# Spreading the shared experts of a scan-and-mixture kernel anew, with a rebuilt head and Silu on ScalarE

## The chip, the cores and the metric

The kernel runs on one core of a Trainium2 chip. The metric is the device time of one execution in microseconds (us), lower is better; a kernel's time is the median of its runs.

## What is computed

Input x has 8 batches of 512 tokens with 256 features, all in fp32. Two layers run one after the other, each followed by the same mixture of experts with the same weights:

```
x = x + scan_layer(layernorm(x))
x = x + mixture(layernorm(x))
x = x + causal_attention(layernorm(x))      # 16 heads of 16, scores clipped to +-10
x = x + mixture(layernorm(x))

scan_layer(x):  xi = silu(x @ Win + bin)                  # 256 -> 512
                h_t = 0.9 * h_(t-1) + xi_t * Bp           # state of 16 per feature
                y = sum_i(h * Cp) + Dp * xi ;  return y @ Wout + bout
mixture(x):     scores = sigmoid(x @ router.T)            # 16 experts in 4 groups
                keep the 2 best groups, then the 4 best experts; weights normalised, times 2.5
                routed = sum over the 4 of weight * down_e(silu(x @ gate_e) * (x @ up_e))
                shared = (silu(x @ sh_gate) * (x @ sh_up)) @ sh_down     # 2 shared experts
                return routed + shared
```

Because the decay is one constant, the scan keeps one state per inner feature and multiplies it by bc = sum(Bp * Cp) afterwards.

## The kernel before

**Stages.** The program has four stretches: the scan layer together with the first mixture's routing and shared experts (`stretch(Scan())`), the routed experts of the first mixture (`routed(0, ...)`), attention with the second mixture's routing and shared experts (`stretch(Attention())`), and the second mixture's routed experts. Between the first two lies no barrier but data: the routed experts need all 4096 tokens sorted into rows by expert.

**A stretch.** `stretch` loops over the batches. In each turn of the loop several pieces of work are written out interleaved, by `beside`: the main work of batch b (for the scan: `Scan.main`), the shared experts of batch b - 2, the routing of batch b - 1 (`Route`), the sends of batch b - 2's tokens, and the norm and transposition of batch b + 1. `beside` weaves pieces by matmul columns; `timed(steps, places...)` puts each step of a piece at a fraction of the turn. The order so written is the order on every engine's queue, and engines run their queues in order. What is listed behind the loop (the rest of the shared experts, the last batch's routing, the table of blocks) makes up the tail of the stretch.

**Scan.main.** For each of 4 chunks of 128 inner features: two matmuls of 512 columns into PSUM (`pz`, L532), sigmoid on ScalarE (L541), times its argument on VectorE (L542), the scan on VectorE (L544), the D skip on ScalarE (L545) and the sum on VectorE (L548). Then `add_projection` multiplies by Wout (`py_s`, L486) and adds to x (L495) in two halves.

**Route.** The norm of batch b (L444, L445; power by GpSimd, L464; rows `sorted_m`, L469), transposition by TensorE (`pt_m`, L406) with copies to `xT_m` (L408), router matmuls (`pl_m`, L630), transposition to `logit_m` (L641), sigmoid (`score_m`, L645), the choice of groups and experts by some forty small VectorE instructions (L656 to L744), counts by matmuls with a triangle and with ones (`pr_m`, L708 and L709), `where_m` (L716), slots cast by ScalarE in pairs (L756; for the last batch by VectorE in one copy, L738) and 16 indirect DMAs from GpSimd that send rows to their places in DRAM (L759). Behind the last batch come the zero fills of the unused ends (16 DMAs on SyncE), and the table of blocks (`pe_b` L871, `pl_b` L880, `lines_b`), which tells `routed` which expert each block of 128 rows has.

**Shared experts.** `shared_experts(i, b, ...)` yields 12 steps per batch: 8 of gate and up (4 matmuls each 128x512 per pair, `pg_m`, L1108), and 4 of down (`pd_m`, L1137); behind each pair come a sigmoid on ScalarE (L1126) and two products on VectorE (L1127, L1128), or a tanh form in attention. `HELD = 6`: in the last turn 6 steps of the batch are issued, the rest behind the loop. The transposed rows `xT_m` live in a pool of nine tiles (tag `kb4`).

**Routed experts.** For each block of 128 rows: gate and up matmuls (`ph`, L994), sigmoid on ScalarE (L1002), two products on VectorE (L1004, L1005), down matmuls (`pyr`, L1025), a gain on ScalarE (L1034) and an indirect DMA that adds the rows to the result (L1035). Expert weights are all resident in one tile, `w_all`, 3072 columns for each of 16 experts; in the scan stretch `later` holds their loads, which are issued on SyncE behind the loads of x.

**Head.** Constants are made by GpSimd; norms 0 and 1 take the inverse root by 13 VectorE instructions of Newton steps (`first`, `pinned`); `first_two` writes out batch 0's and batch 1's chunks. `load_shared` loads the shared weights.

Of the kernel before, what the change touches and what calls it, by code (L numbers as in the profile page):

```python
# [15 lines left out]
P = 128  # L16
# [47 lines left out]
HELD = 6  # L64
AHEAD = 6
BY_PE = 3

# [15 lines left out]
def tile_hybrid_block(  # L83
# [88 lines left out]
    load_x(0)  # L172
    ident = const.tile([P, P], FP, name="ident")
    make_identity(nc, ident)

# [13 lines left out]
    nc.scalar.dma_start(out=w_out_sb, in_=w_out.rearrange("(c p) d -> p c d", p=P))  # L189
    b_out_sb = const.tile([P, D], FP, name="b_out_sb")  # L190
    nc.gpsimd.dma_start(out=b_out_sb, in_=b_out.partition_broadcast(P))
    load_x(1)

    rw_sb = const.tile([P, KD, SQ], FP, name="rw_sb")
    nc.gpsimd.memset(rw_sb, 0.0)
    nc.gpsimd.dma_start(out=rw_sb[:, :, 0:E], in_=router_t.rearrange("(p k) e -> p k e", p=P))
    rb_sb = const.tile([P, E], FP, name="rb_sb")
    nc.gpsimd.dma_start(out=rb_sb, in_=route_bias.partition_broadcast(P))
# [24 lines left out]
    def load_expert(e: int):  # L223
# [11 lines left out]
    nc.gpsimd.memset(before, 1.0)  # L235
    nc.gpsimd.affine_select(
        out=before,
        in_=before,
        compare_op=ALU.is_gt,
        fill=0.0,  # L240
        base=0,
        pattern=[[1, EG], [-1, EG]],
        channel_multiplier=0,
    )
    neg_half = const.tile([P, NT], FP, name="neg_half")
    nc.gpsimd.memset(neg_half, -0.5)
# [4 lines left out]
    nc.scalar.activation(begun, decay, AF.Sigmoid)  # L251
# [6 lines left out]
    def load_attention_weights():  # L258
# [14 lines left out]
    nc.gpsimd.memset(causal, TOP)  # L273
    nc.gpsimd.affine_select(
        out=causal, in_=causal, compare_op=ALU.is_ge, fill=0.0, base=0, pattern=[[0, 2], [1, P]], channel_multiplier=-1
    )
# [3 lines left out]
    nc.gpsimd.memset(tri, 1.0)  # L280
    nc.gpsimd.affine_select(
        out=tri, in_=tri, compare_op=ALU.is_gt, fill=0.0, base=0, pattern=[[1, P]], channel_multiplier=-1
    )
    ones = const.tile([P, P], FP, name="ones")
    nc.gpsimd.memset(ones, 1.0)
# [4 lines left out]
    for e in range(E):  # L290
        nc.gpsimd.memset(region[:, e : e + 1], float(e * REG))
    steps = const.tile([P, NJ], FP, name="steps")
    nc.gpsimd.iota(steps, [[BLK, NJ]], base=0, channel_multiplier=0, allow_small_or_imprecise_dtypes=True)
# [29 lines left out]
    nc.gpsimd.memset(zeros, 0.0)  # L323
    nc.gpsimd.iota(zeros[:, D + 2 * TK :].bitcast(I32), [[0, SAME]], base=NTOK, channel_multiplier=1)


    later = [lambda e=e: load_expert(e) for e in range(E)]
# [62 lines left out]


# [45 lines left out]
    def normed(b: int, tag: str, place, by_vector: bool = False, pinned: bool = False, past=lambda: None):  # L437
# [10 lines left out]
        if by_vector:  # L448


            var = small.tile([P, NT], FP, tag="var", name=f"var_{tag}", bufs=1)
            keep(nc.vector.tensor_scalar(var, mv[:, :, 1], EPS, None, ALU.add))
            bits = small.tile([P, NT], I32, tag="bits", name=f"bits_{tag}", bufs=1)
            keep(nc.vector.tensor_scalar(bits, var.bitcast(I32), 1, None, ALU.logical_shift_right))
            keep(nc.vector.tensor_scalar(rstd.bitcast(I32), bits, -1.0, HALVED, ALU.mult, ALU.add))
            off = small.tile([P, NT], FP, tag="off", name=f"off_{tag}", bufs=1)
            for _ in range(3):
                keep(nc.vector.tensor_mul(off, rstd, rstd))
                keep(nc.vector.scalar_tensor_tensor(off, off, -0.5, var, ALU.mult, ALU.mult))
                keep(nc.vector.scalar_tensor_tensor(rstd, off, 1.5, rstd, ALU.add, ALU.mult))  # L460
            yield
        else:
            nc.vector.tensor_scalar(rstd, mv[:, :, 1], EPS, None, ALU.add)
            nc.gpsimd.tensor_tensor(rstd, rstd, neg_half, ALU.pow)  # L464
# [33 lines left out]
    class Scan:  # L498
        mixture, ahead, copies, turns = 0, 1, by_scalar, (0.75, 0.79)
        early = 0  # L500
# [5 lines left out]
        def load(self, b: int):  # L506
            if b + 1 < B and b > 0:
                with tc.issue_after(load_x(b + 1).ins):
                    for load in later[b - 1 :: shares]:
                        load()  # L510

# [12 lines left out]
        def main(self, b: int, xnT):  # L524
            tag = f"s{b}"

            def steps():
                y_sb = []
                for c in range(NI):
# [11 lines left out]
                    nc.scalar.activation(xi, pz, AF.Sigmoid, bias=bias)  # L541
                    nc.vector.scalar_tensor_tensor(xi, pz, bias, xi, ALU.add, ALU.mult)  # L542
# [38 lines left out]

    class Route:
# [3 lines left out]
        def __init__(self, i: int, b: int, copies):  # L586
            self.i, self.b, self.tag, self.copies = i, b, f"m{i}_{b}", copies
            self.held = {}
            self.rest = choices(i, b, self.tag, self.held, b < B - 1)
# [17 lines left out]
        def scores(self, shares: bool = False):  # L607
            if shares:
# [9 lines left out]
                self.copies,  # L618
                past=wide if self.i == 0 and self.b == B - 2 else None,
# [275 lines left out]
    def routed(i: int, table, beside):  # L895
# [90 lines left out]
        def up(n: int):  # L986
# [15 lines left out]
            nc.scalar.activation(act, ph[0], AF.Sigmoid)  # L1002
            with tc.issue_after(turns.pop(n + 1).ins) if n + 1 in turns else nullcontext():
                nc.vector.tensor_mul(act, ph[0], act)  # L1004
            made = nc.vector.tensor_mul(act, ph[1], act)  # L1005
# [43 lines left out]
        def run(first: int, last: int):  # L1049
# [13 lines left out]
            nc.scalar.activation(primed, decay, AF.Sigmoid)  # L1063
# [29 lines left out]
    def shared_experts(i: int, b: int, xnT_of, tanh: bool):  # L1093
# [3 lines left out]
        def steps():  # L1097
            xnT = xnT_of()
            acts = []
            for n in range(NSH):  # L1100
# [3 lines left out]
                for f in range(KF):  # L1104
# [20 lines left out]
                    else:  # L1125
                        nc.scalar.activation(sig, ph, AF.Sigmoid)  # L1126
                        nc.vector.tensor_mul(sig, ph, sig)  # L1127
# [35 lines left out]
    class Attention:  # L1163
        mixture, ahead, copies, turns = 1, 2, by_both, (0.65, 0.85)
        early = 2
        norms, scores, choose = (0.0, 0.12, 0.2, 0.28), (0.29, 0.45, 0.55, 0.6), (0.66, 0.95)
        last_rows, last_scores = (0.2, 0.28), (0.35, 0.38)
        bursts, parts = {}, {}

# [210 lines left out]
    def stretch(layer):  # L1380
# [5 lines left out]
        def norm(b: int, first: bool = False):  # L1386
# [4 lines left out]
            return normed(b, f"l{i}_{b}", place, first, first)  # L1391
# [13 lines left out]
        def experts(b: int):  # L1405
            return shared_experts(i, b, lambda: routes.pop(b).held["xnT"], i == 1)

        for b in range(layer.ahead):
            if b < layer.early:
                xT[b] = ready.pop(b)  # L1410
            else:
# [3 lines left out]
                issue(Piece(0, turn(b, by_both if first else layer.copies)))  # L1415
                if first:
                    load_shared()
            if b == 0:
                issue(project(b))

        def first_two():

            layer.load(1)
            issue(Piece(0, norm(1, True)))
            for _ in range(2):
                pending.pop(0)()
            main = layer.main(0, made.pop(0))
            issue(Piece(0, some(main.steps, NI)))
            issue(Piece(0, turn(1)))
            issue(project(1))  # L1430
            second = layer.main(1, made.pop(1))
            issue(Piece(0, some(second.steps, NI)))
            issue(main)
            return Piece(second.columns - NI * KD * T, second.steps)
# [9 lines left out]
        for b in range(1 if begun else 0, B):  # L1444
            pieces = [begun or layer.main(b, made.pop(b))]
            begun = None
            nxt, last = b + layer.ahead, b == B - 1
            fill = []
            if layer.ahead > 1 and not last:
                fill.append(project(b + 1))  # L1450
            if b > 1:
                shared_sum = experts(b - 2)
                if last:

                    each = shared_sum.columns // 12
                    rest = Piece((12 - HELD) * each, shared_sum.steps)

                    many = HELD * each if layer.mixture else HELD * each * 3 // 2
                    shared_sum = Piece(many, some(shared_sum.steps, HELD))
# [4 lines left out]
            if b > 0:  # L1464
# [13 lines left out]
                else:  # L1478
                    pieces += [
                        timed(r.scores(i == 1), *layer.scores[:2], *spread(*layer.scores[2:], NT)),  # L1480
                        timed(some(r.rest, PICKS), *spread(*layer.choose, PICKS)),
                    ]
            if nxt < B:
                added = layer.load(nxt)
                if added is not None:
# [4 lines left out]
                    timed(turn(nxt), *layer.turns),  # L1490
# [4 lines left out]
            if i == 0 and b == 2:  # L1495
# [10 lines left out]
                behind(rest, experts(B - 2)),  # L1506
# [9 lines left out]
                experts(B - 1),  # L1516
# [104 lines left out]
```

## Time and profile before

| what | us |
|---|---|
| median of 3 runs (lowest, highest) | 1681.23 (1679.09, 1684.41) |
| the profiled execution: its time | 1674.03 |
| its span, first to last instruction | 1672.1 |
| first matmul of a routed expert | 366.87 |
| scan stretch, 80 to 240 us: busy time of TensorE, VectorE, ScalarE, GpSimd per 40 us | 40.0, 34.6, 12.1, 23.7 |
| attention stretch with its tail, 745 to 1278 us: TensorE busy | 498.08 |
| second routed stretch, 1278 to 1660 us: TensorE busy | 378.08 |

PE is TensorE's matmuls, PEld its weight loads, DVE VectorE, ACT ScalarE, POOL GpSimd, SP SyncE, which only starts DMAs. A busy PE is one that has matmuls in flight. A wait is put down to the instruction whose semaphore came last. The granted clock is the share of full speed that the throttle left to TensorE. The four values of the fourth row are means of the four windows from 80 to 240 us.

### The profile page before, as it was taken

Reading aid. Unit: us, or ns where it says so; the run is one execution under the profiler, and the core shown is the slowest. Engines: PE = TensorE matmul, PEld = TensorE weight load, DVE = VectorE, ACT = ScalarE, POOL = GpSimd, SP = SyncE. Lnnn points to the kernel's source line nnn. Section 1 sums busy time; section 2 is a strip of 40 time slices with the busy share of each in tenths; the row PEclk is TensorE's granted clock in tenths of the full one; section 3 lists DMA queues with packets and bytes.
Section 4 is the critical chain, followed back from the end, with each engine's and each line's share of the span. In section 5 each row is a group of like instructions: output and inputs, shape, how many; then the busy total and the mean of one; then the engine's idle time right before and its main releaser. Section 6 shows DMA issues by size and latency. Waiting matters only on the chain.

```text
span 1672.1 us, 34224 instructions
## 1 busy us (share of the span) xinstructions
PE 1572.9 (94%) x9992; PEld 1156.6 (69%) x9992; DVE 1159.7 (69%) x3623; ACT 745.4 (45%) x1461; POOL 758.1 (45%) x655
## 2 busy tenths in 40 slices
PE   6999996979999999999999999999787999999996
PEld 3566663659999999984444454454356999999996
DVE  7988876436677766656888978978754566666664
ACT  3222332125555555546544443444213555555553
POOL 3365663525555555550023423422552555555554
PEclk9999998989999999999999999999899999999998
DMA  5354431527777766641333423332643767777776
GB/s 166 127 192 170 135 110 60 186 75 106 107 124 122 104 99 99 99 57 42 89 93 107 121 85 117 96 96 90 210 170 72 110 113 113 137 136 136 134 135 133
DMA packets 281645, 195.31 MB, mean 117 GB/s; under 512 B 168592, under 2 KB 262064, under 8 KB 281456
## 3 DMA queue, kind: packets, MB, share of 16 engines
q1 hardware_dynamic: 228368, 119.40, 27.9%
q0 software_dynamic: 51984, 72.09, 23.9%
q8 instruction: 85, 1.39, 0.3%
q10 hardware_dynamic: 1104, 1.57, 0.3%
q14 instruction: 104, 0.85, 0.2%
HBM read 89.71 MB, written 103.23 MB: 115 GB/s over the span
## 4 chain that ended last, share of the span: by engine, by line
PE 38%; DVE 9%; DMA 3%; issue 1%; ACT 1%; another core or an unknown queue 0%; DVEq 0%; POOLq 0%; SPq 0%; ACTq 0%
PE ph L994 13%; PE pyr L1025 6%; PE ps_a L1244 4%; PE pd_m L1137 3%; DMA part<-rows 3%; PE pq_a L1192 2%; PE po_a L1280 2%; PE pg_m L1108 2%; PE py_a L486 2%; PE pv_a L1210 1%; DVE w_all L1264 1%; DVE w_all L1265 1%; DVE act_m L1124 1%; ACT w_all L1254 1%; DVE sig_m L1123 1%
## 5 line engine op out<-in xcount | busy, mean ns | idle before, releaser
L1035 POOL DMA_INDIRECT part<-rows x272 | 426.3, 1567 | 339.7 <-ACT rows L1034 252.3
L759 POOL DMA_INDIRECT xg<-sorted_m,slots_m x256 | 258.6, 1010 | 293.7 <-ACT slots_m L756 78.0
L994 PEld LDWEIGHTS ph<-rows,gate 128*128 128x128 f32 x2160 | 277.8, 191 | 33.4 <-ACT rows L977 21.6
L994 PE MATMUL ph<-rows,gate 128*128 128x128 f32 x2160 | 291.5, 278 | 1.9 <-ACT rows L977 1.9
L994 PE MATMUL ph<-rows,up 128*128 128x128 f32 x2160 | 285.3, 275 | 0.0
L1025 PE MATMUL pyr<-w_all,rows 128*128 x1088 | 279.2, 380 | 0.0
L967 DVE COPY up<-w_all 128x512 f32 x270 | 118.8, 441 | 211.4 <-PE ph L994 191.6
L994 PEld LDWEIGHTS ph<-rows,up 128*128 128x128 f32 x2160 | 262.9, 192 | 0.0
L967 ACT COPY gate<-w_all 128x512 f32 x270 | 166.5, 618 | 122.3 <-DVE up L967 55.7
L1254 ACT ACTIVATE w_all<-ps_a 128x1024 f32<-128x1024 f32 x160 | 155.2, 1021 | 108.5 <-PE ps_a L1244 101.0
L1025 PEld LDWEIGHTS pyr<-w_all,rows 128*128 128x128 f32 x1088 | 186.9, 192 | 14.3
L1034 ACT ACTIVATE rows<-pyr,gain 128x256 f32<-128x256 f32 x272 | 128.9, 474 | 80.9 <-PE pyr L1025 60.1
L1002 ACT ACTIVATE rows<-ph 128x256 f32<-128x256 f32 x272 | 104.6, 384 | 114.3 <-PE ph L994 99.5
L1004 DVE TENSOR_TENSOR rows<-ph,rows 128x256 f32<-128x256 f32 x272 | 115.1, 423 | 31.7 <-ACT rows L1002 27.7
L1005 DVE TENSOR_TENSOR rows<-ph,rows 128x256 f32<-128x256 f32 x272 | 115.2, 424 | 26.2 <-issue 0.9
L1137 PE MATMUL pd_m<-sd_sb,act_m 128*128 128x256 f32 x512 | 122.8, 386 | 7.8 <-DVE act_m L1124 7.7
L1108 PE MATMUL pg_m<-xT_m,sg_sb 128*128 128x512 f32 x256 | 123.3, 604 | 0.0
L1108 PE MATMUL pg_m<-xT_m,su_sb 128*128 128x512 f32 x256 | 122.5, 600 | 0.0
L1137 PEld LDWEIGHTS pd_m<-sd_sb,act_m 128*128 128x128 f32 x512 | 96.4, 192 | 31.3 <-DVE act_m L1124 9.3
L1244 PE MATMUL ps_a<-w_all 32*128 32x384 f32 (+3 forms) x1024 | 104.7, 475 | 14.0 <-ACT w_all L1254 13.9
L1264 DVE SCALAR_TENSOR_TENSOR w_all<-w_all,causal 128x512 f32<-128x512 f32 (+1 forms) x160 | 91.8, 574 | 33.3 <-ACT w_all L1254 31.2
L1244 PEld LDWEIGHTS ps_a<-w_all 32*128 32x128 f32 x1024 | 45.2, 190 | 69.6 <-ACT w_all L1254 39.1
(213 smaller groups left out, 1960.3 us busy)
## 6 DMA issues: line engine op xcount, KB each, us to landing
rows<-xg SPq DMA_DIRECT2D x720, 32.0 KB
rows<-xg SPq DMA_DIRECT2D x92, 134.0 KB
part<-x SPq DMA_DIRECT2D x16, 512.0 KB
part<-ys_m SPq DMA_DIRECT2D x14, 512.0 KB
sum<-part SPq DMA_DIRECT2D x14, 512.0 KB
w_all<-in_L_ffn_gate_w_dram SPq DMA_DIRECT2D x27, 256.0 KB
w_all<-in_L_ffn_up_w_dram SPq DMA_DIRECT2D x27, 256.0 KB
w_all<-in_L_ffn_down_w_dram SPq DMA_DIRECT2D x27, 256.0 KB
```

The lines of the kernel that those rows point to most:

```text
L759: nc.gpsimd.indirect_dma_start(out=xg[i], out_offset=bass.IndirectOffsetOnAxis(ap=slots[:, at : at + 1], axis=0), in_=rows[:, t, :], in_of ...
L967: copy(here, w_all[:, bass.ds(held[n][0] + half * KD * F, KD * F)])
L994: nc.tensor.matmul(ph[s][:, f * P : (f + 1) * P], lhsT=both[s][:, k * F + f * P : k * F + (f + 1) * P], rhs=rows[:, ROW + k * P : ROW + (k ...
L1004: nc.vector.tensor_mul(act, ph[0], act)
L1005: made = nc.vector.tensor_mul(act, ph[1], act)
L1025: nc.tensor.matmul(py, lhsT=act[:, f * P : (f + 1) * P], rhs=w_all[:, bass.ds(w + 2 * KD * F + f * D, D)], start=(f == 0), stop=(f == KF - 1),
L1034: nc.scalar.mul(y, py, gain[:, TK : TK + 1])
L1035: acc = nc.gpsimd.indirect_dma_start(out=parts[i][n % 2], out_offset=bass.IndirectOffsetOnAxis(ap=rows[:, D + 2 * TK : D + 2 * TK + 1].bit ...
L1108: made = nc.tensor.matmul(dst, lhsT=w[:, k, f * P : (f + 1) * P], rhs=xnT[:, k, :], start=(k == 0), stop=(k == KD - 1),)
L1137: nc.tensor.matmul(py[:, j, :], lhsT=acts[n][:, f, t * P : (t + 1) * P], rhs=shared[n][3][:, f, :], start=(n == 0 and f == 0), stop=(n == ...
L1244: nc.tensor.matmul(ps[j // 2][:, j % 2, col : col + n], lhsT=k_sb[w][r, o, c * P : (c + 1) * P], rhs=q_sb[r, o, c * P : T], start=True, st ...
L1254: nc.scalar.activation(es[two], ps[two], AF.Exp, scale=ATT_SCALE)
```

## The change

- **Shared experts.** One generator, `all_experts`, runs through the shared experts of all batches, and each turn takes a number of steps from it (`quota`). In the scan stretch this is 10 in turns 2 to 6, 10 in turn 7, 20 in the first part behind the loop, and the remaining 16 in the last part (before: 12, 6, 18, 12). In attention the numbers are as before (12, 6, 18, 12).
- **Rows.** The shared experts so fall up to three batches behind, and `xT_m` must stay longer. For batches 0 to 5 of the first mixture it is kept in three slots (`kept_rows`) in the place of experts 14's and 15's weights in `w_all`. Those two are loaded by `done_with` once batch 5's shared experts are issued.
- **Head.** Norms 0 and 1 use the GpSimd power. Constants that are needed later (`late`) are made behind batch 1's power; 16 memsets of `region` become one iota; the Wout load moves from ScalarE's queue to SyncE behind x of batch 1. 14 idle matmuls stand ahead of the first transposition, and 5 between the projections of batch 0 and the rest. Two chunks of batch 0 come ahead of batch 1's transposition, where before it was four. In turn 1 the scores and choices of batch 0 move to the end of the turn (0.95 to 0.99, before 0.53 to 0.97), and the transposition of batch 2 to 0.96.
- **Silu.** Sigmoid and product become one Silu on ScalarE in the scan, in the first mixture's shared experts and in both routed stretches. The router's scores of the first mixture keep Sigmoid. As built, the program has 20 loads of ScalarE's function table, before it had 4.
- **Slots.** The last batch of the first mixture gets its slots cast by ScalarE in pairs too.

```diff
-HELD = 6
+OUT, STAY = 2, 3
+IDLE, FIRST = 14, 2
...
-    nc.scalar.dma_start(out=w_out_sb, in_=w_out.rearrange("(c p) d -> p c d", p=P))
     load_x(1)
+    nc.sync.dma_start(out=w_out_sb, in_=w_out.rearrange("(c p) d -> p c d", p=P))
...
-    for e in range(E):
-        nc.gpsimd.memset(region[:, e : e + 1], float(e * REG))
+    nc.gpsimd.iota(region, [[REG, E]], base=0, channel_multiplier=0, allow_small_or_imprecise_dtypes=True)
...
-    later = [lambda e=e: load_expert(e) for e in range(E)]
+    later = [lambda e=e: load_expert(e) for e in range(E - OUT)]
...
+    def keep_busy(many: int, name: str):
+        idle = bank([P, P], f"idle_{name}")
+        for _ in range(many):
+            nc.tensor.matmul(idle, lhsT=ones, rhs=ones, start=True, stop=True)
...
     class Scan:
+        quota = (10, 10, 20)
+        def done_with(self, b: int):
+            if b == B - 3:
+                for e in range(E - OUT, E):
+                    load_expert(e)
...
-                    nc.scalar.activation(xi, pz, AF.Sigmoid, bias=bias)
-                    nc.vector.scalar_tensor_tensor(xi, pz, bias, xi, ALU.add, ALU.mult)
+                    nc.scalar.activation(xi, pz, AF.Silu, bias=bias)
...
+    def kept_rows(b: int):
+        at = (E - OUT) * WEXP + b % STAY * KD * T
+        return w_all[:, at : at + KD * T].rearrange("p (k t) -> p k t", k=KD)
...
-            self.rest = choices(i, b, self.tag, self.held, b < B - 1)
+            self.rest = choices(i, b, self.tag, self.held, i == 0 or b < B - 1)
...
+                home=(lambda _: kept_rows(self.b)) if self.i == 0 and self.b < B - 2 else None,
...
-            nc.scalar.activation(act, ph[0], AF.Sigmoid)
+            nc.scalar.activation(act, ph[0], AF.Silu)
             with tc.issue_after(turns.pop(n + 1).ins) if n + 1 in turns else nullcontext():
-                nc.vector.tensor_mul(act, ph[0], act)
-            made = nc.vector.tensor_mul(act, ph[1], act)
+                made = nc.vector.tensor_mul(act, ph[1], act)
...
-                        nc.scalar.activation(sig, ph, AF.Sigmoid)
-                        nc.vector.tensor_mul(sig, ph, sig)
+                        nc.scalar.activation(sig, ph, AF.Silu)
...
-            return normed(b, f"l{i}_{b}", place, first, first)
+            return normed(b, f"l{i}_{b}", place, False, first)
...
-        def experts(b: int):
-            return shared_experts(i, b, lambda: routes.pop(b).held["xnT"], i == 1)
+        def all_experts():
+            for b in range(B):
+                yield from shared_experts(i, b, lambda: routes.pop(b).held["xnT"], i == 1).steps
+                layer.done_with(b)
+        whole = all_experts()
+        each = NSH * KF * (2 * KD * T + NT * D) // 12
+        def experts(many: int):
+            return Piece(many * each, some(whole, many))
+        if i == 0:
+            keep_busy(IDLE, "head")
...
-            issue(Piece(0, norm(1, True)))
+            second = norm(1, True)
+            issue(Piece(0, some(second, NT)))
             for _ in range(2):
                 pending.pop(0)()
+            issue(Piece(0, second))
+            load_shared()
+            with tc.issue_after(powers["l0_1"].ins):
+                for make in late:
+                    make()
+            layer.load(1)
+            with tc.issue_after(powers["l0_1"].ins):
+                issue(project(0))
             main = layer.main(0, made.pop(0))
-            issue(Piece(0, some(main.steps, NI)))
+            issue(Piece(0, some(main.steps, FIRST)))
             issue(Piece(0, turn(1)))
+            issue(Piece(0, some(main.steps, NI - FIRST)))
...
+            keep_busy(5, "between")
...
+            scores, choose, turns = layer.scores, layer.choose, layer.turns
+            if i == 0 and b == 1:
+                scores, choose, turns = (0.95, 0.955, 0.97, 0.975), (0.98, 0.99), (0.96, 0.965)
...
-                shared_sum = experts(b - 2)
+                shared_sum = experts(layer.quota[last])
...
-                behind(rest, experts(B - 2)),
+                experts(layer.quota[2]),
...
-                experts(B - 1),
+                Piece((B * 12 - (B - 3) * layer.quota[0] - sum(layer.quota[1:])) * each, whole),
```

## The prediction

> **What bounds the kernel now.** I read the page first: the span, the busy shares and the 40 slices (41.8 us each).
>
> ```profile
> span 1672.1 us, 34224 instructions
> ...
> PE 1572.9 (94%) x9992; PEld 1156.6 (69%) x9992; DVE 1159.7 (69%) x3623; ACT 745.4 (45%) x1461; POOL 758.1 (45%) x655
> ...
> PE   6999996979999999999999999999787999999996
> ...
> PEclk9999998989999999999999999999899999999998
> ```
>
> TensorE is busy 94% of the span. Its row falls below 9 in slice 1 (the head), slices 7 to 9, and slice 32, which the diff does not reach. So I read the slices up to 9, the scan stretch, which ends where the first matmul of a routed expert starts (366.87 us). The windows (columns: window, length, busy time of PE, PEld, DVE, ACT, POOL, then granted clock, DMA share, GB/s):
>
> ```profile
> 40.00:80.00 40.00, 37.17 (x140) 22.66 (x139) 37.10 (x121) 12.36 (x25) 10.43 (x13) 0.96 0.32 110
> ...
> 120.00:160.00 40.00, 40.00 (x174) 25.71 (x173) 33.27 (x99) 11.88 (x27) 23.41 (x26) 1.00 0.52 178
> ...
> 240.00:280.00 40.00, 31.13 (x119) 18.50 (x118) 27.00 (x79) 11.28 (x27) 22.80 (x25) 0.97 0.27 95
> 280.00:320.00 40.00, 30.71 (x113) 19.95 (x114) 21.85 (x105) 5.41 (x17) 17.72 (x20) 0.82 0.35 118
> 320.00:360.00 40.00, 29.62 (x101) 17.57 (x100) 13.65 (x42) 4.34 (x8) 15.53 (x16) 0.87 0.38 127
> 360.00:400.00 40.00, 38.86 (x281) 36.56 (x280) 21.67 (x74) 19.84 (x44) 14.92 (x11) 1.00 0.60 100
> ```
>
> From 80 to 240 us PE is busy 40 of 40 us and everything else has slack (DVE 33 to 36 us, POOL 24, ACT 12): there, less PE work is less time, and less DVE work is nothing. From 240 to 360 PE idles 28.5 us and the clock falls to 0.82: there a chain of small steps on other engines sets the end. Ten-microsecond windows put the half clock right behind the idle: 0.53 at 285 to 295, 0.63 at 345 to 355. The waits of PE up to 367 us (total, times, longest):
>
> ```profile
> PE pr_m L708 <- DVE sel_m L700: 14.7, 1, 14.7
> PE pt_l L406 <- DVE xn L469: 11.4, 4, 9.3
> PE pe_b L871 <- DVE chosen_b L860: 10.4, 1, 10.4
> ```
>
> Two of them, pr_m and pe_b, are the tail's. The first on DVE's own timeline, then the second on PE's:
>
> ```profile
> 274.11 0.29 DVE L677 SCALAR_TENSOR_TENSOR s_m<-sel_gm,s_m 128x64 f32<-128x64 f32 x1
> 284.41 0.69 DVE L495 TENSOR_TENSOR x<-py_s,x 128x512 f32<-128x512 f32 x1 [10.01 <-remote]
> ```
>
> ```profile
> 333.36 1.88 PE L1108 MATMUL pg_m<-xT_m,sg_sb 128*128 128x512 f32 x4
> 335.07 1.88 PE L1108 MATMUL pg_m<-xT_m,su_sb 128*128 128x512 f32 x4
> 336.79 1.88 PE L1108 MATMUL pg_m<-xT_m,sg_sb 128*128 128x512 f32 x4
> 349.05 2.28 PE L871 MATMUL pe_b<-chosen_b,cand_e 128*128 128x143 f32 x8 [10.38 <-DVE chosen_b L860]
> ```
>
> L495 adds a scan result, py_s7_0, whose matmuls end at 273.18 by the record, yet DVE starts it at 284.41 and names no releaser in the trace; all of the last batch's routing stands behind it. Before the second wait ScalarE (L1126) stands 7.2 us and DVE (L1128) 4.6 us in the same way. What delays these is not in the trace; I carry it as an unknown. The last block also gives the size of a step of shared experts: groups of 4 matmuls start 1.72 us apart (333.36, 335.07, 336.79).
>
> **The change part by part.**
>
> *Shared experts spread anew.* Eight batches have 12 steps each, 96 in all. Before, loop turns 2 to 6 take 12 each, turn 7 takes 6, the stretch after the loop 18, the last 12. Now 10, 10, 20 and 16. So 5 x 2 = 10 steps leave the stretch in which PE is full, and 4 + 2 + 4 enter the tail. Middle: 10 x 1.72 = -17.2 us, if PE stays the bound: a turn goes from 37.5 us (copies of xT_l at 93.76, 131.09, 168.55, 206.10, 243.54) to 34.05. Per turn DVE has about 32 us now and loses its L542 and L1127 (4 x 0.74 + 4 x 0.68 = 5.7, the second in proportion to the steps); POOL has 23.7 x 37.5/40 = 22; both fit. The next x tile is fetched when sorted rows are done (116.37) and first read some 14 us later, so the shorter turn has room for its 4 us of landing. Tail: +17.2 us of work on PE, against the idle there: 14.66 + 10.38 + 1.41 + 1.2 + 0.68 = 28.3 us. In the changed order the shared steps stand between the last logits and pr_m (about 10 us of them), and 25.8 us of them between pr_m and pe_b, where the chain (where, slots, 16 sends at 1.27) needs about as much. I take the two large waits as filled to 1.41 + 0.68 = 2.1 us, which any order leaves: -26.2; and the half-clock stretches behind them (277.34 to 294.41, in which 6.4 us are busy, and 349.05 to 352.44) give back 3.2 + 1.7 = 5 us. Tail 17.2 - 26.2 - 5.0 = -14.0. If the unknown delays stay in full and the filler is spent ahead of them, 10.0 + 4.6 of it is lost: -14.0 to +0.6. I take -14.0, since both waits are seen only where PE has nothing queued, and now it has.
>
> *Rows kept in two experts' places.* xnT of batches 0 to 5 goes into the place of weights 14 and 15 in three slots. A slot is overwritten three batches later; at ten steps a turn batch b's gate and up matmuls are done in turn b x 1.2 + 2, rounded up, about one turn ahead of that. The six weight loads (0.4 to 1.3 us of SP each) now wait on SP for the shared matmuls of batches 3 to 5; behind them in SP stand x_7's store, ys stores, and the 16 zero fills with which the last sends begin (320.5). The last awaited matmul comes in the 20 steps after the loop, ahead of those fills. Nothing if so; a late one delays the sends by what it is late, 0 to 5 us.
>
> *Head.* The first two norms lose 13 DVE steps to one power on POOL (L464, 1.04 and 1.13 us in its two groups), constants on POOL move behind it, w_out goes from ScalarE's queue to SP behind x_1 (w_out landed 15.2, first used at 36.95: nothing). xn_0 starts at 8.71 now, about 7.4 then. xn_1 (23.5 now) waits only for x_1's landing at 12.2: four stats, power, rows, 18.6. Then DVE sets the pace, 1.22 + 0.72 + 0.75 = 2.7 us a chunk of eight: x_0's add at 38.7 instead of 42.67, -4.0. But route 0's choice now stands at the end of turn 1, behind the stats of the next x tile, which lands 4.2 us after x_0's store: PE is out of work from about 55.1 to 60.8. Net, beside the two steps counted above, -0.6. Bounds: -4.0 if that wait is covered, +5 if a half-clock stretch of the kind at 52.06 to 55.48 follows it as well. I take -0.6. The 14 idle matmuls lie in PE's empty first 9.3 us; the 5 others stand where DVE sets the pace, and without that cover cost 5 x 0.28 (a 128x128 matmul, as L994 has it).
>
> *Sigmoid and product become Silu.* 272 routed products (L1004, 0.423 us: 115 us of DVE) lie beside a full PE (360 to 400 us: PE 38.9 of 40, DVE 21.7): 0, at most -0.4 for each stretch's last block. L1002's own 0.384 us is taken as unchanged. But router scores keep Sigmoid, and the built program reloads ScalarE's table around each of the eight scores of this stretch, 16 loads more:
>
> ```profile
> L541 ACT ACTIVATE xi_s<-pz_s,b_in_sb 128x512 f32<-128x512 f32 x32 | 21.9, 684 | 31.2 <-PE pz_s L532 25.7 <-DVE y_s L548 5.5
> ...
> L645 ACT ACTIVATE score_m<-logit_m 128x64 f32<-128x64 f32 x8 | 2.1, 259 | 26.5 <-issue 17.8 <-DVE logit_m L641 8.8
> ...
> L251 ACT ACT_TABLE_LOAD x1 | 1.3, 1283 | 2.8 <-issue 2.8
> ```
>
> A load is 1.283 us. Sixteen on the path would be 20.5. In the middle ScalarE is busy 12 of 40 us, so they hide, and would cost 2.6 us per turn without that cover; only the last score lies on the tail's chain: +2.6 (0 to 20.5).
>
> The Trainium skill, "ScalarE: Activation LUTs", section "What ACT_TABLE_LOAD costs", gives 1283 ns for the load and about 1380 ns of drain, 2.66 us a switch. The three loads here agree with the first figure; none of their rows shows a drain. By the page, 16 switches are an estimated 42.6 us of ScalarE, and the sum's last term would be 5.3.
>
> *Sum:* -17.2 - 14.0 - 0.6 + 2.6 = -29.2. The profiled execution took 1674.03 us (2 us around its span) and would take 1644.8; the median shown lies 7.2 above it, so I forecast 1681.2 - 29.2 = **1652** for the median.
>
> **The rivals.**
> *B, the delays stay* (10.0 and 4.6 us, or a chain as long): -29.2 + 14.6, **1667**. For it: they have no cause in the trace. Against: none is seen in the full windows.
> *C, the middle does not shrink*: a queue keeps the turn at 37.5; -29.2 + 17.2, **1669**. Against: DVE's 6 us of slack grows.
> *D, the scores hold the path (slower)*: ScalarE, in order, stands at each score for the logit (26.5 us over eight, 3.3), then 0.26, and two loads 2.57: 6.1 us in which the next scan chunk's xi and every PSUM bank behind it wait. If PE and DVE have no cover, 8 x 6.1 = 49, against -31.8 without loads: +17, **1698**. It decides from 31.8/8 = 4.0 us a score. For it: the scan chain crosses ScalarE twice a chunk. Against: today's 3.6 us per score leaves PE at 40 of 40. The skill's drain (same page and section) would make a switch pair alone 5.3 us, past that point.
> *E, no change* (B and C together, or the head's wait doubled): about **1681**.
>
> **How the numbers follow.** Forecast 0.47, B 0.19, C 0.12, D 0.14, E 0.08. About 0.3%, 5 us, can be told from no change: faster is below 1676, slower above 1686. Faster 0.47 + 0.19 + 0.12 and a little of E = 0.80; same 0.06; slower 0.14. The forecast's own range is 1643 to 1662 (the head's +-4.5, the loads' 0 to 5, half of the unknown delay). For 8 in 10 it reaches to B, C and E: 1640 to 1684, leaving D and a better tail outside.
>
> **What would show it.** Right: PE 40 of 40 with xT_l copies 34 us apart in turns 3 to 6; first routed matmul near 335; pr_m's and pe_b's waits under 2 us; clock near 1.0 from 240 to 360; twenty table loads, none with PE idle beside it; the routed stretch as long as before. Wrong: copies still 37 apart (C), x's add long after its py (B), a gap on PE at each score (D), or more than 6 us of idle at pr_m in the head.

## The result, and the profile after

Four runs of the changed kernel have a median of 1664.36 us (1659.38 to 1667.46), beside 1680.62 for the kernel before (1679.09 to 1684.41): a ratio of 0.9898, 95% interval 0.9883 to 0.9913. That is 16.3 us faster: inside the wide range of 1640 to 1684, above the forecast's own 1643 to 1662, and little more than half of the 29.2 us that were forecast. It is close to rival B's time (1667). The profile's head, slices and clock:

```profile
span 1661.7 us, 33893 instructions
...
PE 1583.4 (95%) x10030; PEld 1162.3 (70%) x10030; DVE 1004.3 (60%) x3265; ACT 766.2 (46%) x1486; POOL 762.9 (46%) x639
...
PE   8899998999999999999999999999888999999996
...
PEclk9999998999999999999999999999899999999998
```

The profiled execution took 1663.38 us. Its first routed matmul starts at 351.37 us instead of 366.87; the forecast's sum would have it near 335. The routed stretches are as long as before (377.2 and 376.3 us, before 377.1 and 376.5, from the first to the last weight load of ph, the routed experts' gate and up matmuls). From the last ph load of the first to the first of the second, attention, it is 538.2 us, before 534.3. But for the order of some slot casts on ScalarE and one copy more on VectorE, the instructions of this piece are those of before, and in the profiles of e1 to e11 below, which leave it as it is too, it lies between 534.4 and 543.3. So spans do not tell 5 us apart here; I compare medians and ratios, and the start of the first routed matmul. The windows (columns as before):

```profile
40.00:80.00 40.00, 33.88 (x139) 19.46 (x137) 32.60 (x114) 13.62 (x26) 14.44 (x18) 0.96 0.43 144
...
120.00:160.00 40.00, 40.00 (x168) 26.80 (x167) 27.73 (x100) 15.10 (x32) 24.55 (x27) 1.00 0.45 157
...
240.00:280.00 40.00, 33.35 (x129) 22.15 (x128) 24.24 (x86) 10.51 (x26) 18.87 (x20) 0.87 0.22 77
280.00:320.00 40.00, 38.53 (x134) 21.37 (x133) 20.01 (x86) 12.62 (x28) 21.86 (x25) 1.00 0.64 209
320.00:360.00 40.00, 38.00 (x182) 27.11 (x181) 11.88 (x37) 10.35 (x24) 8.62 (x10) 1.00 0.34 92
360.00:400.00 40.00, 40.00 (x302) 37.96 (x301) 19.77 (x69) 22.02 (x49) 23.20 (x15) 1.00 0.72 107
```

The tail's idle time is largely gone (240 to 360 us: PE 109.9 of 120, before 91.5), but the clock is 0.87 from 240 to 280. Waits of PE up to 370 us:

```profile
PE pr_m L743 <- DVE sel_m L735: 11.4, 2, 6.6
PE pd_m L1170 <- DVE act_m L1161: 5.0, 2, 2.6
PE pt_l L431 <- DVE xn L494: 4.0, 4, 2.7
```

pe_b no longer waits, pr_m still does, and pd_m is new: it waits in turns that had no wait before. What is behind both is on VectorE's timeline, first in turn 2, then in the tail:

```profile
75.79 1.37 DVE L494 TENSOR_SCALAR xn<-x,mv_l,rstd_l 128x256 f32<-128x256 f32 x4
86.62 0.32 DVE L676 STREAM_TRANSPOSE logit_m<-pl_m 128x128 f32<-128x128 f32 x1 [9.46 <-remote]
88.12 0.69 DVE L520 TENSOR_TENSOR x<-py_s,x 128x512 f32<-128x512 f32 x1 [1.18 <-remote]
```

```profile
261.71 0.15 DVE L719 MAX8 best_m<-s_m 128x8 f32<-128x16 f32 x1
267.81 0.69 DVE L520 TENSOR_TENSOR x<-py_s,x 128x512 f32<-128x512 f32 x1 [5.94 <-remote]
```

VectorE stands 9.46 and 5.94 us and names no releaser. In turn 2 it waits for pl_m, whose matmuls had started at 79.39. Behind that wait stands the product act_m for which pd_m waits, so now TensorE is held too, and the half clock behind it stretches one half of py_s to 3.23 us, where the group before it at 84.47 took 1.89:

```profile
79.39 0.64 PE L665 MATMUL pl_m<-w_all,rw_sb 128*32 128x128 f32 x16
...
90.77 0.70 PE L1170 MATMUL pd_m<-sd_sb,act_m 128*128 128x256 f32 x2 [2.37 <-DVE act_m L1161]
91.31 3.23 PE L511 MATMUL py_s<-w_scan,y_s 128*128 128x256 f32 x8
```

Columns of a timeline: start, time, engine, line, operation, tiles, number; in brackets the idle time before it and what ended it. All 16 extra table loads are there, and take 1.283 us each:

```profile
L680 ACT ACT_TABLE_LOAD x8 | 10.3, 1283 | 0.1
...
L1160 ACT ACT_TABLE_LOAD x6 | 7.7, 1283 | 9.2 <-PE pg_m L1142 8.1 <-issue 1.1
...
L572 ACT ACT_TABLE_LOAD x2 | 2.6, 1283 | 0.0
```

### The profile page after: what moved, and what is told of

It reads as the page before. It is cut to its first block, busy times and chain, and to the rows that moved or that the text cites. A ratio compares the mean times of both kernels' runs of the same rounds, so it can differ in the third digit from the quotient of the medians.

```text
span 1661.7 us, 33893 instructions
## 1 busy us (share of the span) xinstructions
PE 1583.4 (95%) x10030; PEld 1162.3 (70%) x10030; DVE 1004.3 (60%) x3265; ACT 766.2 (46%) x1486; POOL 762.9 (46%) x639
## 3 DMA queue, kind: packets, MB, share of 16 engines
q10 hardware_dynamic: 576, 1.05, 0.2%
## 5 line engine op out<-in xcount | busy, mean ns | idle before, releaser
L1039 DVE TENSOR_TENSOR rows<-ph,rows 128x256 f32<-128x256 f32 x272 | 115.3, 424 | 151.3 <-ACT rows L1037 80.9
L1301 DVE SCALAR_TENSOR_TENSOR w_all<-w_all,causal 128x512 f32<-128x512 f32 (+1 forms) x160 | 91.5, 572 | 38.3 <-ACT w_all L1291 36.4
L1317 PE MATMUL po_a<-w_all,v_a 128*32 128x512 f32 (+3 forms) x1024 | 92.8, 452 | 0.3 <-issue 0.3
L1016 DVE STREAM_TRANSPOSE rows<-rows 128x256 f32<-128x256 f32 x180 | 78.8, 438 | 5.6 <-issue 2.6
L1142 PE MATMUL pg_m<-xT_m,sg_sb 128*128 128x512 f32 x160 | 78.0, 610 | 0.0
```

The lines of the kernel that those rows point to most:

```text
L1317: nc.tensor.matmul(at["po", w][32 * j : 32 * j + 32, c * P : T], lhsT=v_sb[:, c, h * VC : h * VC + 32], rhs=at[w, c, j], start=(c == place ...
```

## The experiments

Medians are of 4 to 7 runs (e5 and e6: one run); each ratio is to runs of the kernel before on the same chip. "Waits" counts those of VectorE of 1 us or more up to 370 us that name no releaser, with the longest. Where it says 0, ScalarE has none either; before it had 6, in the changed kernel 4.

| | median | ratio (95%) | first routed matmul | waits, longest |
|---|---|---|---|---|
| before | 1680.62 | 1 | 366.9 | 2, 10.0 |
| changed | 1664.36 | 0.9898 (0.9883 to 0.9913) | 351.4 | 6, 9.5 |
| e1 no sends | 1645.02 | 0.9795 (0.9775 to 0.9815) | 332.7 | 0 |
| e2 quota back | 1658.16 | 0.9875 (0.9856 to 0.9894) | 351.1 | 2, 1.8 |
| e3 tanh scores | 1657.58 | 0.9873 (0.9855 to 0.9891) | 347.6 | 2, 7.4 |
| e4 head alone | 1673.26 | 0.9972 (0.9953 to 0.999) | 359.7 | 4, 4.1 |
| e5 adds, no sends | 1790.05 | one run | 475.5 | 0 |
| e6 thin sends | 1673.51 | one run | 355.0 | 4, 9.6 |
| e7 tanh, quota back | 1664.23 | 0.9904 (0.9887 to 0.992) | 348.9 | 2, 4.5 |
| e8 Silu alone | 1673.77 | 0.9962 (0.9947 to 0.9977) | 363.8 | 8, 17.4 |
| e9 spaced sends | 1651.63 | 0.9824 (0.9808 to 0.9841) | 336.5 | 0 |
| e10 spaced, tanh | 1651.71 | 0.983 (0.9802 to 0.9858) | 336.6 | 0 |
| e11 spaced, quota back | 1656.57 | 0.9851 (0.9833 to 0.9868) | 345.4 | 0 |
| e12 spaced, both mixtures | 1645.55 | 0.9785 (0.9767 to 0.9803) | 342.3 | 0 |

The theory came from where the late waits fall. GpSimd's timeline beside the 5.94 us wait shows sends without a pause:

```profile
256.96 0.96 POOL L794 DMA_INDIRECT xg<-sorted_m,slots_m  x1 [0.30 <-issue]
258.22 0.96 POOL L794 DMA_INDIRECT xg<-sorted_m,slots_m  x1 [0.30 <-issue]
259.48 0.96 POOL L794 DMA_INDIRECT xg<-sorted_m,slots_m  x1 [0.30 <-issue]
```

There are 16 of them from 250.53 to 271.82. The trace's record of TensorE's semaphore, though not every count is in it, has none between 256.96 and 267.79.

### e1: no sends

```diff
+                if i == 0:
+                    yield
+                    continue
                 free(f"xg{i}", nc.gpsimd.indirect_dma_start(...))
```

(and zero rows from SyncE into the regions that the routed experts read)

> The changed kernel without the indirect sends of the first mixture: none of GpSimd's 128 transfers to xg is issued, and SyncE writes about as many bytes of zero rows there in 31 plain transfers, so the first mixture's routed part comes out as zero. Theory L (dense sends hold back TensorE's finished signals, and that is where the missing 13 us went): the waits of the changed kernel that name no releaser (VectorE 9.46 us at 86.6, 5.94 at 267.8, 3.93 at 274.3; ScalarE 16.43 at 274.2) shrink to under 1 us each, the 2.4 us wait of pd_m at 90.8 and the 6.65 us wait of pr_m at 270.4 to under 2 us, and the first routed matmul comes 8 to 16 us earlier, at 335 to 343 instead of 351.4. Rival (TensorE's results are late for a reason of its own, such as its clock or its idle time): the waits stay within 2 us of these sizes, and the first routed matmul within 4 us of 351.4.

No wait of 1 us or more without a releaser is left up to 370 us, and the routed stretch starts at 332.73 us, 18.6 ahead of the changed kernel and 2.3 ahead of the forecast's sum without the loads (366.87 - 31.8 = 335.1). The waits of PE in this run:

```profile
PE pr_m L761 <- DVE sel_m L753: 5.8, 2, 5.0
...
PE pd_m L1191 <- DVE act_m L1182: 1.4, 1, 1.4
```

The 5.0 is the head's, where route 0's choice was forecast to leave 5.7; pr_m's second is 0.88. So the missing time hangs on the sends. That GpSimd is also free here for its powers and additions is not told apart by this run alone.

### e2: the old numbers of steps

```diff
-        quota = (10, 10, 20)
+        quota = (12, 6, 18)
```

> The changed kernel with the old numbers of steps, 12, 6, 18 and 12, all else as changed. Theory (the trace's account: the new spread gave 9 us in the middle turns and the rest of the gain in the tail): 10 to 16 us more than the changed kernel, 1674 to 1680. By the forecast's two terms in full (17.2 and 14.0): 31 us more, 1695. Rival (the head and Silu carry the gain): under 5 us more, and turns 3 to 6 still 37.5 us long.

A miss for all three: 6.2 us less than the changed kernel by the medians, 3.9 by the ratios, whose intervals overlap. Turns 3 to 6 are 37.5 us again (xT_l copies at 87.25 and 237.35), so the spread does shorten the middle: 230.18 instead of 237.35. But the tail then takes it back: from there to the first routed matmul it is 113.7 us with the old numbers, 121.2 with the new ones. So the routed stretch starts at the same time (351.1 and 351.4), and in the profiles most of what e2 gains lies behind it, in attention (534.4 us against 538.2), which its edit leaves alone. The steps that the spread moves into the tail find less idle time to fill than was forecast: from the last batch's pt_l to the first routed matmul TensorE idles 14.1 us in e2, where it idled 29.2 before the change. Most of it is in two windows:

```profile
240.00:280.00 40.00, 31.77 (x112) 18.92 (x111) 24.88 (x93) 13.57 (x26) 21.22 (x22) 0.89 0.27 95
280.00:320.00 40.00, 35.56 (x124) 20.39 (x123) 19.55 (x86) 9.14 (x23) 19.71 (x22) 0.94 0.51 164
```

### e3: scores by tanh, 4 table loads instead of 20

```diff
-            nc.scalar.activation(score, pl, AF.Sigmoid)
+            nc.scalar.activation(score, pl, AF.Tanh, scale=0.5)
+            nc.vector.tensor_scalar(score, score, 0.5, 0.5, ALU.mult, ALU.add)
```

> The changed kernel with the first mixture's scores as 0.5 tanh(l/2) + 0.5, tanh on ScalarE and one more VectorE step each, which takes the program from 20 table loads to 4. Theory (the loads lie beside TensorE's work, but for the last scores'): 0 to 3 us less, 1661 to 1665. Rival (16 loads of 1.283 us hold the path, directly or by making the shared products late): 6 us less or more than that, 1658 or under, and the turns with a pd_m wait shorten to 34.1 us.

6.8 us less than the changed kernel by the medians, the rival's number, but 4.2 by the ratios, whose intervals overlap. pd_m still waits (4.9 us the longest), and in e10, where no result is late, the same edit gains nothing.

### e4: the head alone

```diff
-OUT, STAY = 2, 3
+OUT, STAY = 0, 3
...
-        quota = (10, 10, 20)
+        quota = (12, 6, 18)
...
-                home=(lambda _: kept_rows(self.b)) if self.i == 0 and self.b < B - 2 else None,
```

(Silu and the slot casts are undone as well)

> The changed kernel with the old spread (12, 6, 18, 12), xT_m in its pool, all 16 experts loaded early, Sigmoid and product everywhere and the old slot casts: what is left of the change is the head. Theory (the trace of the changed kernel: what the head gains is spent on the wait for route 0's choice and the clock behind it): 1678 to 1682, no change. Rival (the forecast's bound without that wait): 4 to 5 us less than before, 1676.

0.9972, some 4.7 us (1.7 to 7.9): the rival's size, but not its place. The head's own gain is spent by turn 6 as forecast: the last batch's first xT_l copy is at 243.81, before at 243.54. The gain came in the tail, which is 7.4 us shorter though its code is that of before: its two late waits were 10.0 and 4.6 us, here they are 0.4 and 4.1.

### e5 and e6: what about the sends does it

```diff
                 if i == 0:
+                    for _ in range(5):
+                        nc.gpsimd.tensor_add(scratch, scratch, scratch)
                     yield
...
-                        out=xg[i],
+                        out=(thin, xg[1])[i],
...
-                        in_=rows[:, t, :],
+                        in_=rows[:, t, 0:few],
```

(the first to e1's code is e5, the other two are e6, with few = 16 in the first mixture)

> As e1 (no indirect sends in the first mixture, zero rows written by SyncE, the first mixture's routed part zero), but GpSimd does five small additions on a scratch tile in place of each send. Theory L in the form that the indirect transfer holds the signals back: no wait without a releaser over 1 us, first routed matmul within 4 us of e1's 332.7. Rival (a busy GpSimd of any kind does it, by its instructions or its share of the memory): the waits of 4 to 10 us come back, first routed matmul at 343 or later.

> As e1, but the indirect sends are issued as in the changed kernel with 16 of the 268 columns of a row, into a DRAM tile that nothing reads (so the first mixture's routed part is still zero): as many instructions and as many row descriptors, 64 bytes in place of 1072. If what counts is that the transfers are issued (descriptors): the waits without a releaser come back at 4 to 10 us, first routed matmul at 346 to 355. If it is the bytes they move: the waits stay under 1 us, first routed matmul at 332 to 338.

e5's time says nothing on either theory: the additions were issued in long rows ahead of the norms' powers, and TensorE waited for those norms:

```profile
PE pt_m L451 <- DVE sorted_m L514: 133.5, 7, 57.6
```

But in two windows, 120 to 140 and 220 to 240 us, TensorE is busy 20 of 20 us beside a GpSimd that is busy 16 of 20 with these additions alone, and no wait of 1 us or more without a releaser appears: a busy GpSimd is not enough. In e6 they are back, with 64 bytes a row instead of 1072, the longest at the same py_s result as before the change:

```profile
272.95 0.69 DVE L540 TENSOR_TENSOR x<-py_s,x 128x512 f32<-128x512 f32 x1 [9.61 <-remote]
```

So it is the indirect transfers themselves, not the bytes that they move; e6 has as many of them as the changed kernel, so it does not tell their issue from their descriptors.

### e7: e2 and e3 together

Both edits above.

> The changed kernel with both the tanh scores of e3 and the old numbers of steps of e2. If their gains (6 to 7 us each against the changed kernel's 1664.4) have separate causes: 1650 to 1654. If both work by the same thing (both take away a TensorE wait behind a late signal in turns 2, 3 and 5): 1656 to 1660.

A miss for both: 1664.23, as the changed kernel, and 6 us above each edit alone by the medians. By the ratios e2 and e3 gain some 4 us and e7 loses 1, so the two gains do not add up. In the profiles the routed stretch of e2, e3 and e7 starts 0.3, 3.7 and 2.4 us ahead of the changed kernel's. This fits edits that only move where sends and results meet, but these three runs do not show it.

### e8: Silu alone

```diff
-                    nc.scalar.activation(xi, pz, AF.Sigmoid, bias=bias)
-                    nc.vector.scalar_tensor_tensor(xi, pz, bias, xi, ALU.add, ALU.mult)
+                    nc.scalar.activation(xi, pz, AF.Silu, bias=bias)
```

(and so in the shared and the routed experts)

> The kernel before with Silu in place of sigmoid and product at its three places, nothing else. By the forecast's term (VectorE's products lie beside TensorE's work, the last score's loads cost 2.6): 1678 to 1683, no gain. Theory from e2 and e4 (e2 has the head, Silu and the slot casts, and starts the routed stretch 8.8 us ahead of the head alone): 5 to 10 us less than before, 1668 to 1673, all of it between the last xT_l and the first routed matmul.

0.9962, 6.4 us less. Where it came from is open: in the profile the first routed matmul is 3.1 us ahead of before, 2.4 of it by the last xT_l, not all behind it.

### e9 and e10: a pause behind each send

```diff
                 free(f"xg{i}", nc.gpsimd.indirect_dma_start(...))
+                if i == 0:
+                    tc.keep_in_program_order(nc.gpsimd.tensor_add(scratch, scratch, scratch))
```

(scratch is 128 x 48; e10 has e3's scores as well)

> The changed kernel, with one small GpSimd addition on a scratch tile (0.27 us) behind each send of the first mixture, so that no two sends follow each other directly; all sends stay, the result is the same. Theory L (signals of TensorE get through only where GpSimd pauses between sends): the waits without a releaser fall to under 2.5 us each (5.94 at 267.8, 9.46 at 86.6 before), pr_m's 6.65 us wait to under 4, and the kernel is 3 to 10 us faster than the changed one, 1654 to 1661, although GpSimd has 4 us more to do per turn. Rival (each send holds signals back for itself, so that pauses change nothing, or the longer row of sends is itself late): 1663 or more, with the waits where they were.

> e9 with the tanh scores of e3. If e9 gains and the causes are separate: 5 to 7 us below e9. If what e3 gained came from how late signals fell and not from the loads: within 3 us of e9.

GpSimd in e9, one addition between two sends:

```profile
256.04 0.99 POOL L797 DMA_INDIRECT xg<-sorted_m,slots_m  x1 [0.17 <-issue]
257.06 0.27 POOL L806 TENSOR_TENSOR scratch<-scratch 128x48 f32<-128x48 f32 x1
257.50 0.98 POOL L797 DMA_INDIRECT xg<-sorted_m,slots_m  x1 [0.17 <-issue]
```

The same addition of py_s to x that stood 5.94 us in the changed kernel, and 10.01 before, now waits 1.05, and for a matmul that the trace names:

```profile
256.90 0.69 DVE L523 TENSOR_TENSOR x<-py_s,x 128x512 f32<-128x512 f32 x1 [1.05 <-PE py_s L514]
```

No late wait is left up to 370 us, the clock is 1.00 from 80 us to beyond the routed stretch's start, and the tail's windows are all but full:

```profile
240.00:280.00 40.00, 38.15 (x163) 23.86 (x163) 26.18 (x97) 14.30 (x34) 30.87 (x47) 1.00 0.42 142
280.00:320.00 40.00, 40.00 (x146) 24.76 (x145) 17.78 (x75) 9.00 (x24) 31.94 (x51) 1.00 0.56 184
```

With more work for GpSimd the kernel became 12.7 us faster than the changed one (1651.63 against 1664.36, and the intervals of the ratios lie apart). e10 gives the same time as e9 (1651.71; their intervals reach some 5 us): with TensorE's signals on time, the 16 table loads cost nothing that these runs can tell, so e3's gain hung on the late signals or on chance. No run tells the pause between two sends from the lower rate of sends, one in 1.46 us in place of one in 1.27.

### e11 and e12: the spread again, and the second mixture

e11: e9 with e2's edit. e12: the addition without its `if i == 0`.

> e9 (a small GpSimd addition behind each send) with the old numbers of steps, 12, 6, 18 and 12. Theory (the spread of the shared experts is worth its forecast once TensorE's signals are on time, less what the tail's chain no longer leaves idle): 6 to 15 us more than e9's 1651.6, 1658 to 1667, against the 6 us less that the same edit made without the additions (e2). By the forecast's two terms in full: 31 us more, 1683. Rival (the spread is worth nothing with or without late signals): within 3 us of e9.

> e9 with the additions behind the sends of the second mixture too. Theory L holds there as well (GpSimd's sends in attention's last turns hold signals back by up to 12 us): 2 to 8 us less than e9, 1644 to 1650, all of it between the first mixture's last matmul and the second's first (541.7 us in e9). Rival (there TensorE has other work while it waits for them): within 2 us of e9.

e11 is 4.9 us above e9 by the medians, 4.5 by the ratios, whose intervals touch (0.9833 to 0.9868 against 0.9808 to 0.9841); the first routed matmul is 9.0 us later, 3.5 of it from the head already (batch 1's pt_l at 18.33 against 14.79, for rows that came later). That is between the rival's 3 and the theory's 6 to 15, and far from 31. e12 is the fastest kernel of this study, 1645.55 us, 6.1 less than e9; its attention piece takes 530.1 us, against 541.7 in e9 and never under 534.3 elsewhere. In that piece e9 still has late waits of VectorE and ScalarE, up to 9.3 us, and TensorE waits 10.5 us for the table of blocks (pe_b); in e12 there is no late wait, and pe_b's wait is under 1.4. (e12's first routed matmul is later than e9's because the head was: the last xT_l copy at 229.86, with a 5.6 us wait for the second batch's rows at 13.5; e11, on the same chip, has 4.5 there, e9 1.4.)

## Why the prediction was right or wrong, point by point

**What bounds the kernel.** Right: TensorE in the middle, a chain of small steps in the tail, and half clock behind each long wait. (The tail's idle time is 29.2 us in the trace, where the prediction adds up 28.3.)

**The tail, -14.0: this is the step that failed.** It came to -5.7 (from the last batch's pt_l transpositions to the first routed matmul 127.6 us before, 121.9 after). pe_b's wait was filled, but pr_m's stayed at 6.65 us, with 10.2 us of half clock behind its start (265.8 to 276.0); the tail's idle time, taken to fall to 2.1 us, fell to 9.6. The prediction carried 0 to 14.6 us for results that come late without a cause in the trace, and took 0, "since both waits are seen only where PE has nothing queued". They are seen there as waits, but the lateness is in the full turns too. A view of the kernel before had it in turns 2 to 6: ScalarE's copy of pt_l, with the transpositions that it waits for below it.

```profile
93.76 0.59 ACT L408 COPY xT_l<-pt_l 128x512 f32<-128x512 f32 x1 [8.10 <-remote]
```

```profile
89.14 1.11 PE L406 MATMUL pt_l<-ident,xn 128*128 128x128 f32 x8
```

The matmuls end by 90.25, the copy starts at 93.76, and so in all five such turns (idle 8.0 to 8.1 us each). It cost nothing as long as TensorE had shared steps queued. e1, e6 and e9 show the cause: sends issued back to back hold it up; without them, or with 0.27 us of other work between them, the same kernel starts its routed stretch at 332.7 and 336.5, and e9 gets back 12.7 of the 12.9 us that were missing. That e9's 1651.6 is the forecast's 1652 is luck all the same: e11, with the old numbers of steps, is already at 1656.6, so most of the gain there is not the spread's.

**The middle, -17.2: about a third of it was the spread's.** The last batch's pt_l starts at 229.50, before at 239.25: 9.8 us with the head's, against 17.8. But from batch 2's pt_l to batch 7's it is 181.8 us, in e2 with the old numbers 187.8: the spread itself gave 6.0. With the sends spaced it gave 11.1 (e9 176.9, e11 188.1). In the changed kernel, from pt_l to pt_l of batches 3 to 7, two turns are 34.1 us as forecast (122.69 to 156.78 and to 190.89), and two are 39.2 and 38.6. Each of these has a wait of pd_m (2.4 and 2.6 us) and 3.4 us of half clock behind it. The forecast asked whether VectorE had time for the shorter turn, not whether the steps still stood where their products were ready: ten steps a turn over a batch of twelve put the down matmuls at another place of each turn. The first of the two waits is a late signal. The second is VectorE's own order: there act_m starts at 216.25 though its gate was ready at 213.1, with other work on VectorE in between, and a wait of 2.2 us stays there in e9 too.

```profile
216.25 0.68 DVE L1161 TENSOR_TENSOR act_m<-pg_m,sig_m 128x512 f32<-128x512 f32 x1
```

```profile
216.98 3.68 PE L1170 MATMUL pd_m<-sd_sb,act_m 128*128 128x256 f32 x10 [2.61 <-DVE act_m L1161]
```

**What the spread is worth.** Forecast at 31 us, it was worth nothing in the changed kernel (e2 is even faster) and about 5 in e9 (e11). The tail's part had the wrong sign: from the last pt_l to the first routed matmul the spread makes it longer, by 7.5 us in the changed kernel (114.4 in e2, 121.9) and by 5.7 in e9 (107.3 in e11, 113.1). The forecast gave the spread all of the 28.3 us idle in the tail to fill. With the old numbers and the rest of the change, the tail idles less: 14.1 us in e2, and 7.9 in e11, where the signals are on time.

**Head, -0.6.** Right by turn 6 (0.3 us later than before by e4, no gain); the wait at pr_m was 4.74 us where 5.7 was forecast. **Silu, 0 and 2.6.** The 272 products in the routed stretches gave nothing, as forecast: both are as long as before. The loads cost less than thought (e10). Of the 2.66 us a switch that the Trainium skill, "ScalarE: Activation LUTs", section "What ACT_TABLE_LOAD costs", gives, this case's traces show the 1.283 us of each load, and no drain beside it: in the changed kernel a load starts 0.02 us behind the instruction before it where nothing else is waited for, and an activation whose input is ready 0.01 us behind the load. That Silu alone gained 6.4 us was not forecast and is not explained.

**Rivals.** B came closest, in time and in kind: results were late, with waits of up to 9.5 us. Its place is right in part only: B left the middle at its full gain and lost 14.6 us in the tail, the runs lost some 8 in each. C (a queue keeps the turn at 37.5) is out: turns of 34.1 are there. D (the scores hold the path) is out: e10. E is out by the interval. The parts do not add up: 4.7 (head), 6.4 (Silu) and -3.9 (spread, e2's ratio) make 7.2 of 16.3; the runs do not split the other 9, and the slot casts and the rows' place were not tried alone. (An expert's weights take 1536 columns of `w_all`, not 3072: two of them make room for the three slots of 1024.)

## What to carry to other kernels

A wait whose releaser the trace does not name is a cost with a cause, also where other work covers it. Before taking such cover away, look at what runs beside all of these waits, in full stretches too, and carry the cost until the cause is found. Where indirect transfers are issued in rows, look whether TensorE's results come late beside them; a few tenths of a microsecond of other work between two of them was worth 12.7 us here, and 18.8 with the second mixture. And where two edits each gain a few us and together nothing, look first whether the gain lies in the stretch that was edited: in its profile, most of e2's did not.

## What the runs showed of the hardware

- Results of TensorE can reach other engines late while GpSimd issues indirect transfers every 1.27 us: by 3.5 us in turns 2 to 6 before the change, with waits up to about 10 in the tail. At 1.46 us apart, with an addition between, no such wait of 1 us or more is left in the first mixture (e9), nor in the second when it is spaced too (e12). What was late is the signal, as far as the record shows: of the pt_l transpositions in turn 2 of the changed kernel, the first four of which started 0.1 us apart from 83.52 on, five counts of TensorE's semaphore stand within 0.2 us, 88.19 to 88.35, some 4 us behind. By what path the issue of a transfer holds signals up is not shown by any run.
- In these traces TensorE's clock falls to half for 3.4 us or a multiple some 2 to 5 us after a wait began: the waits that began at 56.0 and 263.8 in the changed kernel had it from 61.0 and 265.8 on, for 3.4 and 10.2 us. Short waits do not always bring it: 2.37 and 2.61 us did in the changed kernel, 2.24 and 1.85 in e9 did not, one of 1.85 in e11 did (at 290.3, half clock from 292.3).
- As built, Silu and tanh need one table set, Silu and Sigmoid two: the traces show 3 loads in e3, with tanh scores, and 19 in the changed kernel (one more than that in each program as built).
